# A transformer block on one core: the second output projection by seven products instead of eight

## The chip, the cores and the metric

The kernel runs on one core of one Trainium2 chip. The metric is the device time of one execution, in microseconds (us). A core has a matrix engine (TensorE, "PE" in the profile; "PEld" is its loading of the stationary operand), a vector engine (VectorE, "DVE"), a scalar engine (ScalarE, "ACT"), a general engine (GpSimd, "POOL") and a queue engine that here only issues transfers (SyncE, "SP"). PE reads from the on-chip memory SBUF and adds into PSUM, eight banks of 2 KB per partition, 128 partitions. [...]

## The reference

One block of a diffusion transformer, batch B = 2, N = 2048 tokens, C = 576 features, 16 heads of 36, hidden width 2304, all in float32. Cut to what matters:

```
mod = silu(c) @ w_ada + b_ada                      # six rows of 576 per sequence
xn  = layernorm(x) * (1 + sc_msa) + sh_msa
q, k, v = split(xn @ w_qkv + b_qkv);  q, k = layernorm per head
o   = softmax(q k^T * 36**-0.5) v                  # N x 576
x1  = x + g_msa * (o @ w_proj + b_proj)            # the output projection: the change is here
h   = gelu((layernorm(x1) * (1 + sc_mlp) + sh_mlp) @ w1 + b1)
out = x1 + g_mlp * (h @ w2 + b2)
```

## The kernel before, in words

The path that runs is block_of_small (the other one, for inputs whose scores may be large, is not taken). It does, for each of the two sequences b in turn, the input stage (q, k, v), the attention (attend, eight pairs of heads p, four blocks of 512 queries qb, four groups of keys g: steps (p, qb, g)), and the output projection (outputs). Then comes the MLP over both sequences: a first product whose inputs are 512 tokens by 576 features at a time, and a second product. Both MLP products already work by Strassen's scheme: a product of two 2 x 2 block matrices is made of seven block products instead of eight, of sums and differences of the blocks.

**The output projection before.** The attention leaves o transposed in SBUF, as held["qo"]: five chunks of features by 2048 tokens. Four chunks have 128 features each, and the last has the remaining 64, stored twice (partitions 0 to 63 and 64 to 127). w_proj lies in wp (four chunks of 128 rows by 576 columns) and wp4 (the last 64 rows: the left 288 columns on partitions 0 to 63, the right 288 on partitions 64 to 127). For a tile of 128 tokens, whole (L403 to L412) makes for each half a of the 576 output columns four matmuls with 128 rows of contraction, moving 288 columns (L406); halved (L414 to L419) makes one matmul of 64 rows per half, on the two halves of the PE array (L417). outputs (L1353) takes the 16 tiles of a sequence in groups of four: whole for two tiles, halved for all four, whole for the other two. Each tile has its own PSUM tile of two banks (pool "s", four buffers, so all eight banks).

Out of PSUM, DVE multiplies the tile by the gate g_msa (L1367, evicted) and adds the residual x1, which lies in DRAM as x + g_msa * b_proj and was put there during the attention (residual_begun, L1341, by GpSimd). The residual comes by a GpSimd-issued load (L1362), is added on DVE (L1380, summed), and goes back by a GpSimd-issued store (L1381). Seven of the eleven tiles "spare" serve as buffers for that, so a load waits for the store of seven tiles before.

**What else runs during the second projection.** The MLP's first product is prepared by a table `between`, keyed by the token tile at which placed(t) runs its entries:

```
for j in range(TPB + 1):
    between.setdefault(2 * j + 6, []).append(... turned_modulated(...))
for i, t in enumerate((6, 8, 10, 12)):
    between.setdefault(t, []).append(weight_sums[i])
    between.setdefault(t + 1, []).append(last_parts[i])
```

turned_modulated works on ACT (L1022, L388, L389) and ends with a subtraction on GpSimd (L390). weight_sums are four DVE operations on whole weight tiles (L1581 to L1584, 128 x 2304 elements); the first waits for weights wb that ACT's queue starts loading (L1565) once the attention's memory is free. last_parts are DVE operations on the last 64 rows (L400, L401, L1577).

**Order.** PE's order is the program's (a manual schedule around the whole block). In the second projection DVE's order is also the program's; ACT, SP and GpSimd are ordered by the scheduler. In attend, DVE, GpSimd and ACT stand in the program's order; hooks, keyed by (p, qb, g), place extra work in it. An engine carries out its own queue strictly in order: an instruction that waits holds all behind it.

**Around the stage.** Before it stand the last accumulations of the attention (L1291), and a last division: a reciprocal of the sums (L1260) that waits for a transfer (den), and a multiplication (L1261). After it, PE goes on with the first MLP product (L1655), whose first matmul waits for the last read of the projection's PSUM tiles; DVE makes token sums (L1625 to L1628).

Of the kernel before, what the change touches and what calls it, by code (L numbers as in the profile page):

```python
# [8 lines left out]
F32 = mybir.dt.float32  # L9
# [3 lines left out]
ALU = mybir.AluOpType  # L13
# [3 lines left out]
P = 128  # L17
# [5 lines left out]
FULL = 4  # L23
# [8 lines left out]
def dit_block(  # L32
# [25 lines left out]
    nc = tc.nc  # L58
    B, N, C = x.shape
# [3 lines left out]
    NT = N // P  # L63
    NPAIR = H // 2
    HALF = C // 2
# [20 lines left out]
    def s_tile():  # L86
        return psum["s"].tile([P, 2, 512], F32, tag="s", name="s")
# [8 lines left out]
    def opened(name, bufs=1, side="left"):  # L96

        stack = ExitStack()
        pool = stack.enter_context(tc.tile_pool(name=name, bufs=bufs, side=side, reuse_waits="tile"))
        return pool, stack.close  # L100

    def opened_psum(**bufs):

        stack = ExitStack()
        for n, count in bufs.items():
            psum[n] = stack.enter_context(
                tc.tile_pool(name=f"ps_{n}", bufs=count, space=PSUM, reuse_waits="tile")
            )
# [14 lines left out]
    def halves(ap):  # L123
        return ap.rearrange("p (a f) -> p a f", a=2)
# [15 lines left out]
    with tc.tile_pool(name="bound", bufs=1, side="right") as bound:  # L140
# [11 lines left out]
        product = bound.tile([1, 1], F32, name="product")  # L152
# [179 lines left out]
    x1_dram = dram.tile([B, N, C], F32, name="x1_dram")  # L332
# [419 lines left out]
    def block_of_small():  # L752
# [552 lines left out]
        def output_weights(b):  # L1305
            pool, close = opened("wp", side="right")
            wp = pool.tile([P, FULL, C], F32, name="wp")
            wp4 = pool.tile([P, 1, HALF], F32, name="wp4")
            nc.sync.dma_start(out=wp, in_=w_proj[0:512, :].rearrange("(k p) f -> p k f", p=P))
            last_chunk(wp4, w_proj, 1, HALF)  # L1310
            return (wp, wp4, gate_rows(pool, 0, b), pool), close


        def rows_begun(tiles):

            st = xs["pool"].tile([P, 2, 6], F32, name="st", bufs=2)
            mv = xs["pool"].tile([P, len(tiles), 2], F32, name="mvs", bufs=1)
            rstd = xs["pool"].tile([P, len(tiles)], F32, name="rstds", bufs=1)

            def load(i):  # L1320
                xt, src, _ = tiles[i]
                not_sooner(xt)
                nc.gpsimd.dma_start(out=xt, in_=src)

            def measure(i):
                for a in range(2):
# [12 lines left out]
            return load, measure, turn  # L1339
# [80 lines left out]
            summed()  # L1420


        close_psum = opened_psum(s=4)
        xnts, turned, loaded = {0: first_modulated()}, {}, {}

# [5 lines left out]
        for b in range(B):  # L1431
            work, close_work = opened("work", side="right")
            with tc.manual_schedule(
                engines={mybir.EngineType.DVE, mybir.EngineType.SP, mybir.EngineType.Pool}
            ):
                left = inputs(b, weights, making, work, xnts, turned, loaded)
            close_weights()
            close_work()
            close_outs = outs_opened()
            att, close_att = opened("att")  # L1440
            close_psum()
            close_psum = opened_psum(b=8)
            km[1] = att.tile([P, N // 2], F32, name="km1")
            qm[1] = att.tile([P, BLK], F32, name="qm1")
            opening = {}

            def ada_opened():
                opening["ada"], opening["close"] = opened("ada_later", 2, side="right")
                opening["was"] = ada_weights(opening["ada"], GATES[0])
                opening["gates"] = gate_biases(opening["ada"], GATES[0], GATES[2])  # L1450

            def ada_gates():
                gates(opening["was"], opening["gates"], *GATES[:2])
                opening["was"] = ada_weights(opening["ada"], LATER[0])
                opening["biases"] = feature_biases(opening["ada"], LATER[0], nc.sync)

            def ada_feature_rows():
                opening["rows"] = feature_rows(opening["ada"], opening["was"], opening["biases"])

            def ada_features():  # L1460
                features(opening["rows"], LATER[1])
                opening["close"]()

            def output_opened():
                opening["wp"] = output_weights(b)

            hooks = {
                (0, 0, 0): lambda: left,
                (4, 0, 1): output_opened,
            }  # L1470
            hooks |= {
                (3 + t // NBLK, t % NBLK, 3): lambda t=t: residual_begun(b, t) for t in range(NT + 1)
            }
            if b + 1 < B:
                begun = [(spare[5 + t], x[b + 1, t * P : (t + 1) * P, :], spare[8 + t]) for t in range(3)]

                def rows_opened():
                    opening["begun"] = rows_begun(begun)
                    for i in range(len(begun)):
                        opening["begun"][0](i)  # L1480

                def rows_turned():
                    opening["turned"] = opening["begun"][2]()

                hooks |= {(7, 1, 1): rows_opened, (None, None, None): rows_turned}
                hooks |= {
                    (7, 2 + i // NG, i % NG): lambda i=i: opening["begun"][1](i) for i in range(len(begun))
                }
# [12 lines left out]
            close_psum()  # L1501
            close_psum = opened_psum(s=4)
            wp, close_wp = opening["wp"]
            if b + 1 < B:
                weights, close_weights, making = kept_weights()
                xnts = {t: input_loaded(opening["turned"][t], nc.sync) for t in range(2)}
                turned, loaded = {2: opening["turned"][2]}, {}
                first = []

                def turned_of(t):  # L1510
                    squares = spare[8 + t % 3]
                    return (lambda x1: first.append(squares_turned(x1, nc.gpsimd, squares))) if t <= TPB else None

                with tc.manual_schedule(engines={mybir.EngineType.DVE}):
                    outputs(b, wp, {12: [lambda: input_modulated(b + 1, xnts[0])]}, spare[:8], turned_of)
# [84 lines left out]
            between.setdefault(t + 1, []).append(last_parts[i])  # L1600
        in_order = tc.manual_schedule(engines={mybir.EngineType.DVE})
        in_order.__enter__()
        outputs(B - 1, wp, between, spare[:7])
        close_wp()
        close_outs()
        close_xs()
# [296 lines left out]
```

## Time and profile before

| | |
|---|---|
| time, three runs | 3149.82 us median (3149.64 to 3151.75) |
| the profiled execution's own time | 3152.0 us |
| span of its instructions | 3150.2 us, 46743 instructions |
| PE busy | 3125.2 us, 99% of the span |
| DVE, ACT, POOL busy | 1515.6 us (48%), 1471.2 us (47%), 664.2 us (21%) |
| granted PE clock | 0.999 of full speed |
| second projection, PE | from 2076.76 to 2148.47 us of the span |
| first matmul of the MLP after it | 2149.36 us |

Read it from PE: it is busy for all but some 25 us of the span, so time is saved by giving PE less to do, and lost by making PE wait. In the trace each float32 matmul stands as two entries, so a count of 64 in a timeline is 32 matmul instructions. A "mean" of a matmul is the length of one that overlaps its neighbours; what a matmul costs is the distance between starts.

### The profile page before, as it was taken

The page shows a single profiled execution, that of the slowest core. Times are in us where ns is not written, and L with a number is a line of the kernel's source. Part 1 is how long each engine was busy: PE and PEld are TensorE (multiplying, and loading weights), DVE is VectorE, ACT ScalarE, POOL GpSimd, SP SyncE. Part 2 cuts the span into 40 slices and gives each one's busy share as a digit, 9 for nine tenths or more (in the row PEclk, how much of TensorE's full clock was granted, in tenths as well). Part 3 has the DMA queues.
Part 4 walks back from the last instruction along what each step waited for, and adds up shares of the span by engine and source line. Part 5 has one row for each costly group of instructions (what it writes and reads, how often), then busy time and mean ns, then how long its engine had stood idle before and what let it go on. Part 6 is the DMA issues. An engine that isn't in the chain of part 4 may idle for free. (4 is left out here: it accounts for less than half of the span.)

```text
span 3150.2 us, 46743 instructions
## 1 busy us (share of the span) xinstructions
PE 3125.2 (99%) x17553; PEld 1862.0 (59%) x17553; DVE 1515.6 (48%) x2181; ACT 1471.2 (47%) x2843; POOL 664.2 (21%) x932
## 2 busy tenths in 40 slices
PE   8999999999999999999999999999999999999999
PEld 5883333333333788633333333368888888777777
DVE  6653443444344556434443444445566554545454
ACT  2326666666666122466666666633555541000000
POOL 4641000011110455200011111013333320112111
PEclk9999999999999999999999999999999999999999
DMA  5753221132221756411122222146554434333331
GB/s 142 179 96 95 78 64 46 54 80 73 65 74 41 244 101 123 88 45 34 44 62 68 81 65 66 56 159 188 166 132 137 136 109 165 106 121 117 117 105 39
DMA packets 300451, 311.94 MB, mean 99 GB/s; under 512 B 178936, under 2 KB 233080, under 8 KB 298104
## 3 DMA queue, kind: packets, MB, share of 16 engines
q1 hardware_dynamic: 252240, 192.19, 21.2%
q0 software_dynamic: 44432, 111.07, 13.3%
q10 hardware_dynamic: 3544, 5.60, 0.5%
q8 instruction: 141, 2.31, 0.3%
q14 instruction: 94, 0.77, 0.1%
HBM read 191.80 MB, written 106.45 MB: 95 GB/s over the span
## 5 line engine op out<-in xcount | busy, mean ns | idle before, releaser
L1232 ACT ACTIVATE pt<-b 128x512 f32<-128x512 f32 x2048 | 1057.6, 610 | 484.2 <-PE b L1241 271.2
L1241 PE MATMUL b<-pt,vt 128*64 128x512 f32 x4096 | 935.0, 598 | 0.0
L1241 PEld LDWEIGHTS b<-pt,vt 128*64 128x64 f32 x4096 | 271.8, 136 | 582.1 <-issue 438.8
L1228 PE MATMUL b<-qm,km 32*128 32x512 f32 x4096 | 571.9, 614 | 1.0 <-issue 1.0
L1291 DVE TENSOR_TENSOR ot<-b,ot 128x512 f32<-128x512 f32 x192 | 132.8, 692 | 617.5 <-PE b L1241 617.5
L1228 PE MATMUL b<-qe,ke 16*128 16x512 f32 x2048 | 422.1, 788 | 0.0
L1101 PE MATMUL s<-wq,xnt 128*128 128x288 f32 x1536 | 404.9, 407 | 2.1 <-ACT xnt L395 2.1
L1228 PEld LDWEIGHTS b<-qm,km 32*128 32x128 f32 x4096 | 192.3, 184 | 276.8 <-ACT pt L1232 215.6
L1815 PE MATMUL s<-ws,as 128*128 128x288 f32 x1440 | 351.8, 406 | 0.0
L1101 PEld LDWEIGHTS s<-wq,xnt 128*128 128x128 f32 x1536 | 281.5, 190 | 64.7 <-ACT xnt L395 1.6
L1815 PEld LDWEIGHTS s<-ws,as 128*128 128x128 f32 x1440 | 273.6, 190 | 75.6
L1260 DVE RECIPROCAL den<-den 128x512 f32<-128x512 f32 x64 | 213.6, 3337 | 11.1 <-DMA den<-den_dram 11.1
L1655 PE MATMUL m<-xnt,wb 128*128 128x256 f32 x864 | 210.4, 379 | 1.6 <-issue 0.9
L1655 PE MATMUL m<-s,wb 128*128 128x256 f32 x864 | 210.0, 379 | 0.0
L1005 POOL DMA_DIRECT2D turned<-squares x212 | 142.5, 678 | 259.0 <-DVE squares L1000 241.0
L1655 PEld LDWEIGHTS m<-s,wb 128*128 128x128 f32 x864 | 164.2, 190 | 22.3
L1228 PEld LDWEIGHTS b<-qe,ke 16*128 16x128 f32 x2048 | 107.8, 184 | 115.9 <-issue 112.0
L1289 DVE COPY ot<-b 128x512 f32<-128x512 f32 x64 | 44.3, 692 | 272.7 <-PE b L1241 272.7
L1655 PEld LDWEIGHTS m<-xnt,wb 128*128 128x128 f32 x864 | 158.9, 190 | 21.3 <-issue 1.3
L1693 ACT ACTIVATE cs<-cs,b_sb 128x512 f32<-128x512 f32 x144 | 98.9, 719 | 111.8 <-DVE cs L1688 85.8
L812 POOL DMA_DIRECT2D km<-qk x56 | 28.2, 503 | 571.7 <-PE b L1228 568.8
L1022 ACT ACTIVATE xnt<-xnt,mod 128x128 f32<-128x128 f32 x244 | 100.4, 481 | 102.1 <-DMA xnt<-turned 94.6
(206 smaller groups left out, 2941.0 us busy)
## 6 DMA issues: line engine op xcount, KB each, us to landing
gelu<-cs SPq DMA_DIRECT2D x144, 256.0 KB
hidden<-gelu SPq DMA_DIRECT2D x16, 2304.0 KB
x_dram<-spare POOLq DMA_DIRECT2D x64, 288.0 KB, 2.5
qk<-turned_qk SPq DMA_DIRECT2D x120, 144.0 KB
qm<-qk SPq DMA_DIRECT2D x256, 64.0 KB
den<-den_dram SPq DMA_DIRECT2D x128, 128.0 KB
turned<-squares POOLq DMA_DIRECT2D x212, 72.0 KB, 2.5
xnt<-turned POOLq DMA_DIRECT2D x54, 256.0 KB, 4.1
```

What stands on the lines that cost most here:

```text
L1005: queue.dma_start(out=by_square[g], in_=squares[g * SQ : (g + 1) * SQ, :].rearrange("p (k j) -> p k j", j=SQ))
L1022: nc.scalar.activation(part, part, AF.Identity, **affine(which, k, b))
L1101: nc.tensor.matmul(out_a, full[:, k, :], wq[:, k, f], start=k == 0, stop=False)
L1228: nc.tensor.matmul(ps, k[r, keys], q[r, :], start=first, stop=not first)
L1232: nc.scalar.activation(pt[:, h, :], banks[2 * c + h], AF.Exp, scale=SCALE)
L1241: nc.tensor.matmul(acc[64 * h : 64 * h + 64, :], vt[:, v0 : v0 + 64], pt[:, h, :], start=pt is pts[0][0], stop=pt is pts[-1][0],)
L1260: nc.vector.reciprocal(den, den)
L1289: nc.vector.tensor_copy(ot, acc)
L1291: nc.vector.tensor_tensor(ot, acc, ot, ALU.add)
L1655: nc.tensor.matmul(out_m[m], wb[:, slot[m], k, f * P : (f + 1) * P], moving[m](k), start=k == 0 and m in (1, 2, 5, 6), stop=k == 1 and m == 1,
L1693: nc.scalar.activation(part, part, AF.Gelu, bias=b1_sb[:, g : g + 1])
L1815: nc.tensor.matmul(ms[m], stationary[m][:, f, :], ws[m][:, f, :], start=(f == 0), stop=(f == HF - 1))
```

## The change

The second sequence's projection (b = 1) is made by outputs_by_pairs instead of outputs; the first sequence's stays as it was.

A pair is two tiles of 128 tokens, a and b, so with the 512 full features in two halves of 256 and the 576 outputs in two halves of 288 there is a 2 x 2 by 2 x 2 block product. It is made of seven products of two matmuls each (14 per pair instead of 16). The 64 last features stay outside the scheme: two tiles of 64 rows in the first two matmuls of a pair (PSUM tiles x and y), and two at its end (PSUM tile z), these with a difference of the two token tiles' last rows. That is again four matmuls of 64 rows per pair.

- **Weights.** pair_weights loads w_proj and the gate at the same step of the attention as before. During attention steps p = 5 and 6 (11 hooks, one operation each), GpSimd multiplies the weights by the gate and makes five sums of weight blocks. The gate is so in the weights, and DVE no longer multiplies by it.
- **Token sums.** pair_summed makes, on GpSimd, five sums or differences of 128 x 256 elements and two of 64 x 128, per pair. Their memory (pair_memory) is one set for even pairs and one for odd, in tiles of the input stage. The sums of pairs 0 and 1 are made in the attention, at steps (7, 2, 3) and (7, 3, 0); those of pair p + 2 within pair p, into the memory that PE is just reading for pair p.
- **Out of PSUM.** Each pair has four PSUM tiles x, y, z, w of two banks. DVE adds their parts into the residual rows in SBUF, eight additions per pair: four of 576 columns and four of 288.
- **Residual rows.** Two token tiles at a time (576 KB), three buffers, so the load for pair p + 2 waits for the store of pair p - 1. GpSimd issues both, in the program's order with the sums: in pair p first the load for p + 2, then the sums for p + 2, then the store of p, which waits for DVE's last addition of pair p.
- **GpSimd's order** in this stage is now the program's, so the subtractions of turned_modulated (L390 before) stand in pairs 3 to 7, ahead of the load.

```diff
+        def pair_summed(dst, p):
+            q00, q01, q10, q11, a, b = pair_blocks(p)
+            for i, one, op, two in (
+                (2, q10, ALU.add, q11),
+                (5, q00, ALU.add, q01),
+                (1, q00, ALU.add, q11),
+                (7, q01, ALU.subtract, q11),
+                (6, q10, ALU.subtract, q00),
+            ):
+                nc.gpsimd.tensor_tensor(dst[i], one, two, op)
+            for r, one, two in ((slice(0, 64), a, b), (slice(64, P), b, a)):
+                nc.gpsimd.tensor_tensor(dst["last"][r], one[r], two[r], ALU.subtract)
...
+        def outputs_by_pairs(b, weights, memory, between, scratch):
...
+            def residual(p):
+                if p < pairs:
+                    rows[p] = scratch[p % len(scratch)]
+                    nc.gpsimd.dma_start(out=rows[p], in_=rows_of(x1_dram, p))
...
+            def product(out, tokens, i, start=True, stop=True):
+                for k in range(2):
+                    nc.tensor.matmul(
+                        out[:, :HALF],
+                        tokens[:, k, :],
+                        sums[i][:, k, :],
+                        start=start and k == 0,
+                        stop=stop and k == 1,
+                    )
+
+            def last_product(out, tokens, a, first=True):
+                r = slice(64 * a, 64 * a + 64)
+                nc.tensor.matmul(out[:, :HALF], tokens[r], last[r], start=first, stop=not first)
+
+            for p in range(3):
+                residual(p)
+            for p in range(pairs):
+                q00, q01, q10, q11, a, c = pair_blocks(p)
+                s = memory[p % 2]
+                x, y, z, w = (s_tile() for _ in range(4))
+                quarters = rows[p].rearrange("p t (a f) -> p (t a) f", a=2)
+                inner, outer = quarters[:, 1:3, :], quarters[:, 0::3, :]
+
+                def added(dst, part, op=ALU.add):
+                    nc.vector.tensor_tensor(dst, dst, part, op)
+
+                placed(2 * p)
+                last_product(x[:, 0, :], a, 1)
+                last_product(y[:, 1, :], c, 0)
+                product(x[:, 0, :], q00, 3, False)
+                product(x[:, 1, :], s[2], 2)
+                added(inner, x[:, :, :HALF])
+                added(quarters[:, 3, :], x[:, 0, :HALF])
+                added(quarters[:, 3, :], x[:, 1, :HALF], ALU.subtract)
+                product(y[:, 0, :], s[5], 5)
+                product(y[:, 1, :], q11, 4, False)
+                added(inner, y[:, :, :HALF])
+                added(quarters[:, 0, :], y[:, 0, :HALF], ALU.subtract)
+                added(quarters[:, 0, :], y[:, 1, :HALF])
+                product(w[:, 0, :], s[1], 1)
+                placed(2 * p + 1)
+                added(outer, w[:, 0, :HALF].unsqueeze(1).to_broadcast([P, 2, HALF]))
+                product(z[:, 0, :], s[7], 7, stop=False)
+                product(z[:, 1, :], s[6], 6, stop=False)
+                last_product(z[:, 0, :], s["last"], 0, False)
+                last_product(z[:, 1, :], s["last"], 1, False)
+                if p >= 1 and p + 2 < pairs:
+                    residual(p + 2)
+                if p + 2 < pairs:
+                    pair_summed(s, p + 2)
+                added(outer, z[:, :, :HALF])
+                nc.gpsimd.dma_start(out=rows_of(x1_dram, p), in_=rows[p])
...
+            if b + 1 == B:
+                hooks |= {
+                    (5 + i // 6, 1 + i % 6 // 2, 1 + i % 2): lambda i=i: opening["wp"][1][i]() for i in range(11)
+                }
+                hooks |= {(NPAIR - 1, 2, 3): lambda: pair_begun(0), (NPAIR - 1, 3, 0): lambda: pair_begun(1)}
...
-        outputs(B - 1, wp, between, spare[:7])
+        with tc.manual_schedule(engines={mybir.EngineType.Pool}):
+            outputs_by_pairs(
+                B - 1, wp, opening["pairs"], between, [held["spare"][:, 2 * i : 2 * i + 2, :] for i in range(3)]
+            )
```

More of the change, by code (lines that the diff above doesn't have):

```diff
@@ L1311, in output_weights, with pair_weights, gated, last_gated @@
             return (wp, wp4, gate_rows(pool, 0, b), pool), close
+        def pair_weights(b):
+            pool, close = opened("wp", side="right")
+            wp = pool.tile([P, FULL, C], F32, name="wp")
+            wp4 = pool.tile([P, 1, HALF], F32, name="wp4")
+            nc.sync.dma_start(out=wp, in_=w_proj[0:512, :].rearrange("(k p) f -> p k f", p=P))
+            last_chunk(wp4, w_proj, 1, HALF)
+            g1 = gate_rows(pool, 0, b)
+            left, right = (wp[:, :, a * HALF : (a + 1) * HALF] for a in range(2))
+            sums = {
+                1: pool.tile([P, 2, HALF], F32, name="sum1"),
+                2: left[:, 0:2, :],
+                3: right[:, 0:2, :],
+                4: left[:, 2:4, :],
+                5: right[:, 2:4, :],
+                6: pool.tile([P, 2, HALF], F32, name="sum6"),
+                7: halves(g1),
+            }
+            def gated(k):
+                nc.gpsimd.tensor_tensor(wp[:, k, :], wp[:, k, :], g1, ALU.mult)
+            def last_gated(a):
+                r = slice(64 * a, 64 * a + 64)
+                nc.gpsimd.tensor_tensor(wp4[r, 0, :], wp4[r, 0, :], g1[r, a * HALF : (a + 1) * HALF], ALU.mult)
+            def combined(i, one, op, two):
+                nc.gpsimd.tensor_tensor(sums[i], sums[one], sums[two], op)
+            making = [
+                *(lambda k=k: gated(k) for k in range(FULL)),
+                *(lambda a=a: last_gated(a) for a in range(2)),
+                lambda: combined(1, 2, ALU.add, 5),
+                lambda: combined(6, 2, ALU.add, 3),
+                lambda: combined(7, 4, ALU.add, 5),
+                lambda: combined(3, 3, ALU.subtract, 5),
+                lambda: combined(4, 4, ALU.subtract, 2),
+            ]
+            return (sums, wp4[:, 0, :]), making, close
@@ new lines, in pair_memory @@
+        def pair_memory():
+            fulls = [xs["pool"].tile([P, FULL, P], F32, name="xnt", bufs=3) for _ in range(3)]
+            fulls += [
+                xt[:, : FULL * P].rearrange("p (k n) -> p k n", k=FULL) for xt in xs["tiles"][:2]
+            ]
+            return [
+                {
+                    **{m: fulls[i][:, 2 * a : 2 * a + 2, :] for m, i, a in places},
+                    "last": xs["tiles"][n][:, FULL * P : (FULL + 1) * P],
+                }
+                for n, places in enumerate((
+                    ((1, 3, 0), (2, 3, 1), (5, 4, 0), (6, 4, 1), (7, 2, 0)),
+                    ((1, 0, 0), (2, 0, 1), (5, 1, 0), (6, 1, 1), (7, 2, 1)),
+                ))
+            ]
@@ new lines, in pair_blocks @@
+        def pair_blocks(p):
+            qo = held["qo"]
+            a, b = (slice((2 * p + i) * P, (2 * p + i + 1) * P) for i in range(2))
+            return qo[:, 0:2, a], qo[:, 2:4, a], qo[:, 0:2, b], qo[:, 2:4, b], qo[:, FULL, a], qo[:, FULL, b]
+        def pair_summed(dst, p):
[10 more added lines that the diff above has]
+                nc.gpsimd.tensor_tensor(dst["last"][r], one[r], two[r], ALU.subtract)
@@ L1420, in outputs, with rows_of, placed @@
             summed()
+        def outputs_by_pairs(b, weights, memory, between, scratch):
+            sums, last = weights
+            pairs = NT // 2
+            rows = {}
+            def rows_of(ap, p):
+                return ap[b, 2 * p * P : 2 * (p + 1) * P, :].rearrange("(t p) c -> p t c", p=P)
+            def residual(p):
+                if p < pairs:
+                    rows[p] = scratch[p % len(scratch)]
+                    nc.gpsimd.dma_start(out=rows[p], in_=rows_of(x1_dram, p))
+            def placed(t):
+                for do in between.get(t, ()):
+                    do()
+            def product(out, tokens, i, start=True, stop=True):
[8 more added lines that the diff above has]
+            def last_product(out, tokens, a, first=True):
+                r = slice(64 * a, 64 * a + 64)
+                nc.tensor.matmul(out[:, :HALF], tokens[r], last[r], start=first, stop=not first)
[35 more added lines that the diff above has]
+                nc.gpsimd.dma_start(out=rows_of(x1_dram, p), in_=rows[p])
@@ L1464, in output_opened, with pair_begun @@
             def output_opened():
-                opening["wp"] = output_weights(b)
+                opening["wp"] = (output_weights if b + 1 < B else pair_weights)(b)
+            def pair_begun(p):
+                if p == 0:
+                    opening["pairs"] = pair_memory()
+                pair_summed(opening["pairs"][p], p)
             hooks = {
@@ L1473, in block_of_small @@
             }
+            if b + 1 == B:
+                hooks |= {
+                    (5 + i // 6, 1 + i % 6 // 2, 1 + i % 2): lambda i=i: opening["wp"][1][i]() for i in range(11)
+                }
+                hooks |= {(NPAIR - 1, 2, 3): lambda: pair_begun(0), (NPAIR - 1, 3, 0): lambda: pair_begun(1)}
             if b + 1 < B:
@@ L1502, in block_of_small @@
             close_psum = opened_psum(s=4)
-            wp, close_wp = opening["wp"]
+            wp, *_, close_wp = opening["wp"]
             if b + 1 < B:
```

## The prediction, made before the changed kernel ran

> **What bounds the kernel now.** I read the page first: the busy line of part 1, then the chain of waits.
>
> ```profile
> PE 3125.2 (99%) x17553; PEld 1862.0 (59%) x17553; DVE 1515.6 (48%) x2181; ACT 1471.2 (47%) x2843; POOL 664.2 (21%) x932
> PE 30%; DVE 0%; ACT 0%; issue 0%
> ```
>
> PE hardly waits anywhere, so only its own work, or a new wait of it, can move the time. Next the timeline of PE around the second projection; columns are start, length, engine, line, operation, count, and idle time before.
>
> ```profile
> 2076.76 8.03 PE L406 MATMUL s<-wp,qo 128*128 128x288 f32 x32 [0.82 <-DVE ot L1291]
> 2084.72 2.21 PE L417 MATMUL s<-wp,qo 64*128 64x288 f32 x16
> 2086.86 15.79 PE L406 MATMUL s<-wp,qo 128*128 128x288 f32 x64
> ...
> 2140.44 8.03 PE L406 MATMUL s<-wp,qo 128*128 128x288 f32 x32
> 2149.36 1.97 PE L1655 MATMUL m<-xnt,wb 128*128 128x256 f32 x8 [0.90 <-issue]
> ```
>
> The stage is packed: from 2076.76 to the MLP's start at 2149.36 are 72.6 us, of which 0.9 is the wait for DVE's last read of PSUM. The price of one entry comes from the chain, where 2016 of the same width follow each other:
>
> ```profile
> 2654.78 488.89 PE s L1815 x2016
> ```
>
> That is 0.2425 us. Entries of 64 rows run two at a time: 16 of them are 8 slots, 1.94 us at that price. A group of four tiles (72 slots, 17.46) takes 2102.58 - 2084.72 = 17.86 us, so going to the 64-row form and back costs 0.4.
>
> Then DVE, GpSimd and the transfers in the same stretch:
>
> ```profile
> 2083.36 3.35 DVE L1260 RECIPROCAL den<-den 128x512 f32<-128x512 f32 x1 [6.65 <-DMA den<-den_dram]
> 2106.07 2.56 DVE L1581 TENSOR_TENSOR wb<-wb 128x2304 f32<-128x2304 f32 x1 [1.24 <-DMA wb<-in_w_dram]
> 2111.66 1.35 DVE L401 TENSOR_TENSOR wr<-spare,wr 64x1152 fp32r<-64x1152 f32 x1
> ```
> ```profile
> 2096.64 1.22 POOL L1381 DMA_DIRECT2D x_dram<-spare  x2 [1.01 <-DVE spare L1380]
> 2104.07 0.54 POOL L1362 DMA_DIRECT2D spare<-x_dram  x1 [6.21 <-DMA x_dram<-spare]
> 2106.15 2.79 POOL L390 TENSOR_TENSOR parts<-tail,parts 128x128 fp32r<-128x128 f32 x1
> 2119.39 1.21 POOL L1381 DMA_DIRECT2D x_dram<-spare  x2 [2.33 <-DVE spare L1380]
> 2122.06 0.54 POOL L1362 DMA_DIRECT2D spare<-x_dram  x1 [1.46 <-DMA x_dram<-spare]
> ```
>
> Three things are to be seen. A reciprocal of the attention falls inside the stage, at 2083. A store lands in some 2.5 us at 2119, but in over 7 while the weights wb load (2096). And a GpSimd subtraction took 2.79 us while DVE added whole weight tiles. Its line gives the usual length, beside GpSimd's 576-wide addition, and two additions out of PSUM on DVE:
>
> ```profile
> L390 POOL TENSOR_TENSOR parts<-tail,parts x32: 447/468/2785, 2081.5 to 2576.6; 128x128 fp32r<-128x128 f32 x32
> L1350 POOL TENSOR_TENSOR spare<-spare x32: 1408/1416/1868, 586.5 to 1980.9; 128x576 f32<-128x576 f32 x32
> L1822 DVE TENSOR_TENSOR y<-y,s 128x288 f32<-128x288 f32 x16 | 7.3, 454 | 66.2 <-PE s L1815 66.2
> ```
>
> **What the Trainium skill says.** GPSIMD Engine Reference, section 3.1: an operation with two inputs runs at about 2.6 cycles an element at 1.2 GHz, so 2.2 ns. The trace agrees: 128 wide 0.46 us, 576 wide 1.41, a slope of 2.1 ns. SBUF — State Buffer, "Who interferes with whom": a DVE operation with two SBUF inputs and a GpSimd operation that reads SBUF shut each other out for a whole instruction; with one operand in PSUM they don't. The 2.79 above agrees; a subtraction lying wholly under an addition out of PSUM (L1115) took 0.46. DMA: Bandwidth & Descriptors, "Anatomy of one DMA": some 2.0 us and bytes at 436 GB/s, an estimate of 3.4 us for 590 KB. The trace's 295 KB took 2.1 to 2.3 us from the end of issue; I take 2.9 for a double one.
>
> **The change, part by part.**
>
> *PE's work.* Per pair 32 slots (14 matmuls are 28 entries, four of 64 rows are 4 slots) take the place of 36. Eight pairs: 256 x 0.2425 = 62.1. The 64-row form stands at a pair's end and the next one's start, so it is entered 9 times: 9 x 0.4 = 3.5. In all 65.6 against 71.4 before: 5.8 saved, if nothing waits.
>
> *Attention.* GpSimd gets eleven weight operations of at most 1.4 us (row L1350) and two sets of sums, ahead of need; the steps are 6 us long and GpSimd is busy 21%. What could cost: an operation with two SBUF inputs on DVE may start up to 1.4 us late, with DVE half idle. I take 0; bounds 0 and +1.
>
> *DVE.* Before, each tile cost two operations of 0.68 (starts of L1367 and L1380), 2.7 per pair. Now four of 576 columns at 0.68 and four of 288 at 0.37, two of which wait for the one before (0.1 each): 4.4 per pair. Pairs 3 to 6 add a weight sum (2.47 between starts) and last_parts (0.69 + 1.38; 1.28 in pair 5): 8.9, over PE's 8.2. All eight PSUM banks are used once per pair, so PE's first two instructions of the next pair wait for the additions out of x and y.
>   - Pair 1: the order of instructions puts the reciprocal ahead of y's third addition. It can't start before 2083.4 (its transfer), so y comes free at 2087.2, where PE asks at 2085.4: 1.9 us lost.
>   - Pairs 3 to 6: the first weight sum stands ahead of x's additions and waits for wb until 2106, where PE began the pair at 2103.6. From there the backlog stays, and GpSimd's sums shut DVE out of its SBUF-only work by up to 0.75 each. Following the queue, PE waits at the head of pairs 5, 6 and 7 for 2.2, 2.3 and 0.7: 5.1 us.
>
> *GpSimd.* A sum of 256 elements is not in the trace; between 0.46 and 1.41, by the slope 0.73, with dispatch 0.75. Bounds: 0.65 and 0.9. A set is 5 x 0.75 + 2 x 0.5 = 4.75. A pair has: load issue 0.6, set 4.75, store issue 0.6, and the next load waits until that store has landed, 2.9: 8.9 us, over PE's 8.2 even with nothing in the way. From pair 3 on comes the subtraction 0.46, and waits behind DVE's weight work of some 2. Followed through: store 0 at 2089.4, load 3 at 2093.1, store 1 at 2098.4 (landing 7 us later, under wb), load 4 at 2106.2, sums 4 held to 2108.6 by the weight sum, load 5 at 2119.1, load 6 at 2130.1, load 7 at 2142.9. The first sum for pair 7 is ready at 2144.3; PE asks at 2142.8: 1.6 us lost. The residual rows themselves come over 4 us before DVE adds them.
>
> *Moved.* ACT's fourth-row work (L389) now waits for GpSimd's subtractions one pair at a time, as they share one tail tile; the wb loads stand ahead of all but one of these waits, so they start as before. The last subtraction for the MLP's first block stands in pair 6 and is in time.
>
> *End.* The MLP's first matmul waits for the last addition, 0.9 as before. The loads that the MLP's first rows need are issued about a microsecond sooner after it; its one wait of 0.55 there may shrink. I take 0, bounds -0.5 and +1.
>
> *Sum.* 65.6 + 1.9 + 5.1 + 1.6 + 0.9 = 75.1 us against 72.6: **2.5 us longer**. The profiled execution took 3152.0, 1.8 more than its span and 2.2 more than the median; nothing outside the span changes, so I add to the median: 3149.8 + 2.5 = 3152.3.
>
> **The rivals.**
>   - *GpSimd keeps up.* If the shutting out costs nothing, or stores land at once, GpSimd never decides, and DVE's backlog is shorter: 1.9 + 1.6 us of waits, 70.0 us, 2.6 saved: 3147.2. For it: GpSimd is 21% busy on the page. Against: the 2.79, and the chain of 8.9 per pair.
>   - *GpSimd's chain sets the pace*, slower: from a sum of about 0.8 us, or a landing of 3.5, each pair from 5 on waits for its sums. With 0.9 per sum the same following gives 79.2 us: 6.6 lost, 3156.4, and more with contention. For it: five rounds in a row, each over PE's 8.2. Against: the sums are made a whole pair ahead.
>   - *Nothing waits.* 65.6 + 0.9, so 6.1 saved: 3143.7. Against it stands the reciprocal's fixed place in DVE's order.
>   - That PE's work isn't less is excluded by the instruction counts.
>
> **How the numbers follow.** The chances: forecast 0.48, GpSimd keeps up 0.27, GpSimd's chain 0.20, nothing waits 0.05. A measurement here can tell some 0.2%, 6.3 us, from no change. Below 3143.5 lies most of the last case, 0.04; above 3156.1 most of the chain case and a little of the forecast, 0.20; between them 0.76. The range 3146.5 to 3157.5 leaves out some 0.1 on each side; the forecast's own is 3149.5 to 3155.
>
> **What would show it.** In the timeline of the changed kernel: 256 slots between about 2077 and 2151; idle PE entries released by DVE at the head of pair 1 (about 2 us) and of pairs 5 to 7; one released by GpSimd in pair 7's second product; the GpSimd sums at 0.73 alone and longer beside the weight sums; loads 13 to 11 us apart. It is wrong if DVE's weight work starts long before or after 2106, if the sums take 0.9 or more, or if PE waits elsewhere.

## The result, and the profile after

The changed kernel takes 3154.11 us (median of 20 runs, 3151.86 to 3156.48); the kernel before, on the same chip, took 3149.51 (20 runs, 3148.12 to 3152.97). The ratio is 1.0015, 95% interval 1.0009 to 1.0020: some 4.6 us slower (2.8 to 6.3), less than the 0.2% that the prediction counted as a change. The forecast was 3152.3. Its size was near, but the traces show that the time was lost in other places than the forecast had it.

The first thing to read is the busy line of part 1 of the changed kernel's page, beside the one shown of before.

```profile
PE 3122.8 (99%) x17521; PEld 1856.8 (59%) x17521; DVE 1541.4 (49%) x2213; ACT 1471.6 (47%) x2843; POOL 719.2 (23%) x983
```

PE has 32 entries less (17553 before), and is busy 2.4 us less. Yet the span is 3152.3 us instead of 3150.2. Where it went is found by cutting PE's timeline at three of its instructions: the first matmul of the attention's scores, the second projection's first matmul, and the MLP's first matmul. What lies ahead of the first cut is left out, since it isn't touched and differs from run to run (the first score came at 240.40 us before and at 239.56 after; in later runs as early as 237.30). These stretches account for 2.93 us of the 4.6; the rest, 1.7, is not explained.

| us of the profiled execution | before | after | difference |
|---|---|---|---|
| first score to the second projection | 1836.36 | 1839.28 | +2.92 |
| second projection to the MLP's start | 72.60 | 71.46 | -1.14 |
| MLP's start to the end | 1000.85 | 1002.01 | +1.16 |
| together | 2909.81 | 2912.74 | +2.93 |

**The second projection is shorter.** PE's timeline of the changed kernel, as before with start, length, engine, line, operation and idle time before:

```profile
2078.84 0.76 PE L1530 MATMUL s<-wp,qo 64*128 64x288 f32 x4 [0.87 <-issue]
...
2088.46 0.75 PE L1530 MATMUL s<-wp,qo 64*128 64x288 f32 x2 [0.70 <-DVE spare L1542]
...
2121.20 0.99 PE L1530 MATMUL s<-wp,qo 64*128 64x288 f32 x4
...
2131.50 0.75 PE L1530 MATMUL s<-wp,qo 64*128 64x288 f32 x2 [0.77 <-DVE spare L1542]
...
2142.60 2.21 PE L1520 MATMUL s<-wp,xnt 128*128 128x288 f32 x8 [0.72 <-POOL xnt L1386]
...
2150.30 1.97 PE L1817 MATMUL m<-xnt,wb 128*128 128x256 f32 x8 [0.93 <-issue]
```

From the first L1520 of one pair to that of the next are 9.61, 8.16, 8.16, 8.16, 8.51, 10.06 and 8.46 us. A pair without a wait takes 8.16, so the heads of pairs 1, 5, 6 and 7 cost 1.45, 0.35, 1.90 and 0.30. (The idle times in brackets are less than that: a break costs PE more than the idle time that the record shows.) Within pair 7 the wait for GpSimd's sum costs 0.99. That is 5.0 us of waits, and 0.93 at the MLP's start.

DVE and GpSimd in the same stretch, the lines that answer to those of before, first DVE:

```profile
2084.75 3.34 DVE L1260 RECIPROCAL den<-den 128x512 f32<-128x512 f32 x1
...
2106.21 2.56 DVE L1740 TENSOR_TENSOR wb<-wb 128x2304 f32<-128x2304 f32 x1 [0.35 <-DMA wb<-in_w_dram]
...
2112.75 1.49 DVE L401 TENSOR_TENSOR wr<-spare,wr 64x1152 fp32r<-64x1152 f32 x1
```

and GpSimd:

```profile
2099.71 0.72 POOL L1569 DMA_DIRECT2D x_dram<-spare  x1
2107.85 0.71 POOL L1512 DMA_DIRECT2D spare<-x_dram  x1 [7.42 <-PE s L1520]
...
2125.87 2.86 POOL L390 TENSOR_TENSOR parts<-tail,parts 128x128 fp32r<-128x128 f32 x1
```

The reciprocal follows DVE's work without waiting for den. The first weight sum finds wb almost there (0.35 us). On GpSimd the second load waits 7.42 us behind the store of pair 1, which lies among wb's loads; the record names a long finished PE operation, since the store's landing was the last of several things that the load waits for. And L390 takes 2.86 us while DVE adds weights, as before.

**The attention of the second sequence is longer.** PE falls behind in three steps of 0.91 us, near 1816, 1841 and 1938 us of the span. The timeline around the second of them, in the changed kernel:

```profile
1834.30 0.57 POOL L1424 DMA_DIRECT2D spare<-in_x_dram  x1 [19.20 <-DVE met L791]
1834.88 1.42 POOL L1427 TENSOR_TENSOR spare<-spare 128x576 f32<-128x576 f32 x1
...
1837.16 2.78 POOL L1333 TENSOR_TENSOR wp<-wp,gate 128x576 f32<-128x576 f32 x2
1837.29 3.21 DVE L1261 TENSOR_TENSOR ot<-ot,den 128x512 f32<-128x512 f32 x1
...
1840.43 0.68 DVE L1291 TENSOR_TENSOR ot<-b,ot 128x512 f32<-128x512 f32 x1
...
1841.16 0.18 PEld L1228 LDWEIGHTS b<-qm,km 32*128 32x128 f32 x1 [0.64 <-DVE ot L1291]
```

And the same place in the kernel before:

```profile
1837.06 0.69 DVE L1261 TENSOR_TENSOR ot<-ot,den 128x512 f32<-128x512 f32 x1
...
1839.02 0.69 DVE L1291 TENSOR_TENSOR ot<-b,ot 128x512 f32<-128x512 f32 x1 [1.26 <-PE b L1241]
```

The reader sees a chain. GpSimd's queue stood at a load until DVE's copy L791, so the weight operations of two hooks had gathered behind it. From there load, addition and store take GpSimd to 1837.16, and the reciprocal ahead of the division takes DVE to 1837.26. So the two weight operations, back to back (x2, 2.78 us), meet the division. DVE's multiplication by the reciprocal, which has two inputs in SBUF, starts at 1837.29 and ends at 1840.50, 0.56 us after the second of them (1839.95): 3.21 us instead of 0.69. Behind it in DVE's queue stands L1291, which empties a PSUM bank; it comes 1.2 us later than before (1840.43 less 1839.02, less the 0.2 us by which this run is behind there), and PE waits for that bank. The same multiplication took 3.23 at 1812.43 and 3.18 at 1933.93, the other two places. Beside a single GpSimd operation of 1.4 us it took 1.82 and 1.89, and PE lost nothing. A fourth place also has two operations in a row:

```profile
1862.01 2.03 POOL L1337 TENSOR_TENSOR wp<-wp,gate 64x288 f32<-64x288 f32 x2
1862.14 1.24 DVE L1261 TENSOR_TENSOR ot<-ot,den 128x512 f32<-128x512 f32 x1
```

The first ends at 1862.82 and the second starts 0.08 us later, at 1862.90. Here the division got in between: it ended at 1863.38, again 0.56 us after the first, and the second operation took 1.14 us for the first one's 0.81. In the other three places the record has the second operation begin 0.04 to 0.07 us before the first one's end.

**The MLP's start is later still.** PE's second block there waited 0.55 us before, for DVE (L1689). Now:

```profile
2166.34 1.99 PE L1817 MATMUL m<-xnt,wb 128*128 128x256 f32 x8 [1.81 <-DVE cs L1851]
```

DVE's queue has the normalization of the next rows (L272 and on) ahead of that L1851. The timeline of the changed kernel shows what it waited for:

```profile
2148.76 9.75 SPq L1887 DMA_DIRECT2D ws<-in_w_dram  x3
...
2151.20 1.12 POOL L984 DMA_DIRECT2D xt<-x_dram  x2
...
2160.79 0.82 DVE L272 BATCH_NORM_STATS2 st<-xt 128x6 f32<-128x288 f32 x2 [8.05 <-DMA xt<-x_dram]
```

The rows xt land 9.6 us after their issue; before, issued at 2151.42, they were there at 2158.59, 7.2 us later. Two things had come ahead of them: three loads of the second MLP weights (ws, 1.33 MB each), which began at 2150.66 before, and a last store that is now 576 KB long.

### The profile page after: what moved, and what is told of

Read it like the earlier page. It is cut to its first block, busy times and chain, and to the rows that moved or that the text cites. A ratio compares the mean times of both kernels' runs of the same rounds, so it can differ in the third digit from the quotient of the medians.

```text
span 3152.3 us, 46789 instructions
## 1 busy us (share of the span) xinstructions
PE 3122.8 (99%) x17521; PEld 1856.8 (59%) x17521; DVE 1541.4 (49%) x2213; ACT 1471.6 (47%) x2843; POOL 719.2 (23%) x983
## 4 chain that ended last, share of the span: by engine, by line
PE 96%; POOL 1%; issue 1%; DMA 1%; DVE 0%; ACT 0%; POOLq 0%; ACTq 0%
PE b L1241 29%; PE b L1228 20%; PE s L1977 16%; PE s L1101 12%; PE m L1817 12%; PE m L1831 2%; PE s L406 2%; PE one L1817 2%; PE s L1103 2%; POOL xnt L1386 0%; PE s L1520 0%; DMA xt<-x_dram 0%; PE s L417 0%; DMA x_dram<-spare 0%; PE b L192 0%
## 5 line engine op out<-in xcount | busy, mean ns | idle before, releaser
L1291 DVE TENSOR_TENSOR ot<-b,ot 128x512 f32<-128x512 f32 x192 | 132.7, 691 | 611.5 <-PE b L1241 611.3
L1424 POOL DMA_DIRECT2D spare<-in_x_dram x32 | 17.5, 548 | 598.7 <-DVE met L791 583.1
```

Of the source, the lines that this page charges most:

```text
L1291: nc.vector.tensor_tensor(ot, acc, ot, ALU.add)
```

## The experiments

Eight kernels were run. In most of them the numbers of lines shift by a few. The table gives the same three stretches for all of them, from each one's profiled execution, and the measured median beside the kernel before on the same chip. (The eight ran on three chips, so the medians are compared with the one in brackets and not among themselves.)

| run | score to projection | projection | MLP to end | together, against before | median (before) | ratio, 95% interval |
|---|---|---|---|---|---|---|
| changed kernel | 1839.28 | 71.46 | 1002.01 | +2.93 | 3154.11 (3149.51) | 1.0009 to 1.0020 |
| e1_weights_spaced | 1836.38 | 72.04 | 1002.82 | +1.42 | 3151.46 (3149.28) | 0.9999 to 1.0015 |
| e2_division_later | 1839.21 | 79.20 | 1002.03 | +10.64 | 3160.37 (3149.28) | 1.0021 to 1.0049 |
| e3_w2_loads_later | 1839.15 | 71.59 | 1000.45 | +1.37 | 3151.27 (3149.28) | 1.0000 to 1.0017 |
| e4_rows_by_SP | 1839.15 | 71.21 | 1002.28 | +2.83 | 3151.85 (3149.28) | 0.9998 to 1.0015 |
| e5_division_later_wb_held | 1839.25 | 76.48 | 1001.85 | +7.77 | 3156.50 (3149.54) | 1.0014 to 1.0034 |
| e6_all_four | 1836.37 | 69.56 | 1000.96 | -2.92 | 3146.41 (3149.54) | 0.9984 to 1.0000 |
| e7_no_weight_sums | 1839.21 | 68.49 | 1003.41 | +1.30 | 3150.44 (3149.54) | 0.9993 to 1.0010 |
| e8_refined | 1836.34 | 67.19 | 1000.82 | -5.46 | 3144.44 (3149.52) | 0.9977 to 0.9990 |

The first stretch tells two values apart, 1836.4 and 1839.2, to 0.1 us. The projection repeats to 0.1 where its code is the same (71.46 and 71.59); the MLP's stretch is less steady (1001.85 to 1003.41 in the kernels that leave its code alone). Against the kernel before, medians and stretches agree within 0.9 us in the eight kernels, and differ by 1.7 in the changed kernel itself. So the verdicts below rest on the stretches and their lines; a median that lies 2 us under the changed kernel's 3154.11 is not yet a gain.

**1. The weight operations one by one.** Each of them gets a write or a read of one element on DVE ahead of it, so GpSimd can't start it before DVE has come to that step, far from the division.

```diff
...
             def gated(k):
+                nc.vector.tensor_copy(met, wp[0:1, k, 0:1])
                 nc.gpsimd.tensor_tensor(wp[:, k, :], wp[:, k, :], g1, ALU.mult)
...
-                    (5 + i // 6, 1 + i % 6 // 2, 1 + i % 2): lambda i=i: opening["wp"][1][i]() for i in range(11)
+                    (4 + (2 + i) // NBLK, (2 + i) % NBLK, 1): lambda i=i: opening["wp"][1][i]() for i in range(10)
```

> GpSimd's eleven weight operations are held one by one until VectorE has passed the second step of a query block (ten places, the two half ones together, from the fourth head pair on), so that none runs beside the division by den. Theory 1: the changed kernel lost 2.7 us in attention because two such operations back to back shut the 0.69 us division out for 3.2 us, three times, and each time PE waited 0.9. Then no division takes over 2.2 us, PE loses under 0.3 us against the kernel before in attention, and the whole is 2.7 us less than the changed kernel: about 3151.4. Rival: it is the mere number of GpSimd operations in attention, wherever they stand; then at least 2 of the 2.7 us stay, about 3153.5 or more.

The stretch took 1836.38 us, the kernel before 1836.36. The division near 1835 in DVE's timeline of this run:

```profile
1834.69 0.69 DVE L1261 TENSOR_TENSOR ot<-ot,den 128x512 f32<-128x512 f32 x1
1836.64 0.69 DVE L1291 TENSOR_TENSOR ot<-b,ot 128x512 f32<-128x512 f32 x1 [1.26 <-PE b L1241]
```

The longest of all 64 divisions was 1.91 us. All the operations are still there, so their number costs nothing; the loss came from where they stood. It is shown: the three steps, 2.75 us of the changed kernel's 2.92 there, are this collision. (The other 0.15 lie near 1303 us, where nothing was changed.) As a whole this kernel wins less than the 2.7 us of the theory: its projection took 0.58 us longer than the changed kernel's and its MLP 0.81, so the three stretches together are 1.5 us shorter. The median agrees with the theory's 3151.4, which the stretches don't. Why part was lost again wasn't followed up.

**2. The last division later.** The prediction had pair 1's wait in DVE's order: the reciprocal ahead of the third addition out of y. Here ot and den of the last query block lie in memory that outlives the attention, and the division is called after y's additions of pair 0.

```diff
-                den = pool.tile([P, BLK], F32, name="den")
+                den = opening["last"][1] if ending(p, qb) else pool.tile([P, BLK], F32, name="den")
...
+        between.setdefault(1, []).extend(opening["rest"])
```

> The last reciprocal and division of the attention are placed after the additions out of y of pair 0 (their two tiles lie elsewhere). Theory 1: the wait at the head of pair 1 goes (its first product now starts 9.6 us after pair 0's, then 8.2), and what follows moves up with it: 1.4 us less than the changed kernel, 3152.7. Rival: the pace of pairs 5 to 7 is set by VectorE's weight sums, which start when wb lands (2106) whatever PE does; then PE comes 1.4 us earlier to pair 5 and waits there 1.4 us longer, and the time doesn't change: 3154.1.

Neither came. The head of pair 1 no longer waits (8.16 us after pair 0's), but PE stands still later in it: pair 2 begins 15.03 us after it, 6.87 more than without a wait. From the timeline of this run:

```profile
2077.01 16.92 ACTq L1731 DMA_DIRECT2D wb<-in_w_dram  x4
...
2078.67 5.27 SPq L1260 DMA_DIRECT2D xt<-den_dram  x2
...
2088.62 3.35 DVE L1263 RECIPROCAL xt<-xt 128x512 f32<-128x512 f32 x1 [5.43 <-DMA xt<-den_dram]
...
2093.51 2.26 PE L1527 MATMUL s<-sum,xnt 128*128 128x288 f32 x4 [3.80 <-DVE spare L1549]
```

The tiles that the division used had been memory of the attention that wb goes into. With them elsewhere, wb's loads (4.7 MB) start at 2077.01 instead of 2095.57, ahead of den; den's issue takes 5.27 us instead of 1.09, and the reciprocal starts 11.9 us after the stage's first matmul (2076.72). In the changed kernel it was 5.9 (2084.75 after 2078.84). A wait on memory had kept a large load out of the way of a small one. Of the 6.87 us some 4.1 are PE's wait for DVE behind that reciprocal. The other 2.8 are PE's clock: the trace has it at 0.50 of full speed from 2092.41 to 2099.24, and the entries of a matmul start 0.48 us apart there instead of 0.24. No such stretch falls into this stage in the changed kernel; what brings it on was not tested.

**3. The same with wb held until den is there.**

```diff
+        def weights_begun():
+            for i in range(4):
+                nc.vector.tensor_copy(wb[0:1, i, 0, 0:1], opening["last"][1][0:1, 0:1])
+            for i, (k, f) in enumerate(((0, 0), (0, 1), (1, 0), (1, 1))):
+                nc.scalar.dma_start(...)
...
+        between.setdefault(1, []).extend([weights_begun, *opening["rest"]])
```

> As e2_division_later, but the loads of wb are held until den has landed, so they don't run ahead of it. Theory 1: the 7.7 us that e2_division_later lost in the stage came from wb's loads, which began 18 us sooner beside den's. Then den lands at about 2084 again, no wait of 3.8 us is left in pair 1, wb lands some 8 us earlier than in the changed kernel (near 2098), the head of pair 1 doesn't wait, and the stage takes 68.5 to 70 us (changed kernel 71.46): 1.5 to 3 us less than the changed kernel in all. Rival: the order of the division is itself what costs (the additions out of w and z stand behind it): a wait of 2 us or more stays in pair 1, and the stage takes 72 us or more.

den landed as expected, the reciprocal started at 2083.59, 6.75 us into the stage, and no wait is left in pairs 1 to 3 (8.16 us each). So the order of the division is not what costs. But the stage took 76.48 us, and what came in is a rival of the prediction, that GpSimd's chain sets the pace:

```profile
2109.55 0.94 POOL L1519 DMA_DIRECT2D spare<-x_dram  x1 [6.80 <-DMA x_dram<-spare]
...
2123.38 1.24 PE L1527 MATMUL s<-wp,xnt 128*128 128x288 f32 x4 [2.09 <-POOL xnt L1393]
...
2126.41 2.29 PE L1527 MATMUL s<-wp,xnt 128*128 128x288 f32 x4 [1.79 <-POOL xnt L1393]
```

The wb loads now lie over the stores of pairs 0 and 1. GpSimd waits 6.7 and 6.8 us for the two to land before it may issue the next load, and its sums stand behind that load. In pairs 4, 5 and 7 PE waits for the sums; in pair 5 a weight sum on DVE (2122.89, 2.89 us) stretches them further, five in 5.82 us instead of 3.47. Pair 5 takes 15.03 us, and some 2.5 of that are again the clock, at 0.50 from 2124.58 to 2131.41.

**4. The loads of ws held.**

```diff
+            nc.vector.memset(ws[m][0:1, 0, 0:1], 0.0)
             nc.sync.dma_start(out=ws[m], in_=quarter.rearrange("(f p) c -> p f c", p=P))
```

> The loads of the second MLP weights (ws), which begin at 2148.8 in the changed kernel, are held one by one behind VectorE's later work. Theory 1: the 1.8 us wait of PE's second block of the MLP comes from the rows xt landing 9.6 us after their issue among these loads; alone they land in some 3, and the wait falls to 0.5 or less: 1.3 to 1.8 us less than the changed kernel, about 3152.5. Rival: the store of 576 KB just ahead of the rows delays them, or they are late for another reason: they land over 8 us after issue and the wait stays at 1.8.

```profile
2154.57 0.82 DVE L272 BATCH_NORM_STATS2 st<-xt 128x6 f32<-128x288 f32 x2 [3.68 <-DMA xt<-x_dram]
```

Issued at 2149.36, the rows are there 5.2 us later, not 9.6, and PE's wait of 1.81 is gone altogether. The stretch from the MLP's start is 1.56 us shorter than in the changed kernel, and 0.40 shorter than in the kernel before. The 5.2 are more than the 3 of the theory; what remains has the 576 KB store ahead of it, and wasn't split further.

**5. Residual rows by SP.**

```diff
-                    nc.gpsimd.dma_start(out=rows[p], in_=rows_of(x1_dram, p))
+                    queue = nc.gpsimd if p < 3 else nc.sync
+                    queue.dma_start(out=rows[p], in_=rows_of(x1_dram, p))
```

> The residual rows of pairs 3 to 7 are loaded by SP's queue instead of GpSimd's, so GpSimd doesn't wait until a store has landed. Theory 1: GpSimd gains some 3 us per pair, the sums of pair 7 are there in time, and the 0.9 us wait in pair 7's second product goes: 0.9 us less than the changed kernel. Rival: VectorE's backlog sets the pace of pairs 5 to 7, and sums that come earlier only meet it elsewhere; the waits at the heads of pairs 5 to 7 and at the MLP's start take up what is won: no change.

The wait in pair 7's product went, as theory 1 has it: from its first to its last matmul the pair took 6.65 us instead of 7.64. But the heads of pairs 5 and 6 now cost 1.57 and 1.45 us instead of 0.35 and 1.90, and the stage took 71.21 us against 71.46. The rival holds for the time: GpSimd's chain wasn't what paced these pairs. (The median is 2.3 us under the changed kernel's, but the three stretches differ by 0.1 in all, so the edit didn't gain that.)

**6. No weight sums.** ScalarE copies a tile where DVE subtracted two, so part of the MLP is computed from other weights.

```diff
-            lambda: nc.vector.tensor_tensor(wb[:, 4], wb[:, 1], wb[:, 0], ALU.subtract),
+            lambda: nc.scalar.copy(wb[:, 4], wb[:, 1]),
...
```

> The four sums of the MLP's weights are left out: ScalarE copies one of the two instead, so the output isn't the reference's. Theory 1: VectorE's backlog in pairs 3 to 7 comes from these sums of 2.5 us. Then the waits at the heads of pairs 5, 6 and 7 (0.35, 1.9 and 0.3 us) go, GpSimd's operations of 1.9 to 3.2 us shrink to the usual length, the sums of pair 7 come in time, and the stage is 3 to 3.5 us shorter than in the changed kernel, near 68. Rival: pairs 5 to 7 wait for GpSimd's chain of sums, stores and loads, not for VectorE: at least half of these waits stays.

The distances of the pairs became 9.61 and then 8.16 five times and 8.26. What these distances lose before pairs 5, 6 and 7, 2.55 us in the changed kernel, is 0.10 here, and the wait within pair 7 fell from 0.99 to 0.47: together 2.97 us of stage. GpSimd's slow operations in these pairs show the cause from the other side. In the changed kernel, in pair 6:

```profile
2134.01 3.18 POOL L1388 TENSOR_TENSOR xt<-qo 64x128 f32<-64x128 f32 x2
```

and the same sums without DVE's weight sums:

```profile
2131.74 0.98 POOL L1388 TENSOR_TENSOR xt<-qo 64x128 f32<-64x128 f32 x2
```

So DVE's weight sums set the pace of pairs 5 to 7, directly, and in pair 7 in part through GpSimd. (The MLP's longer stretch in this run, 1003.41, wasn't followed up.)

**7. Together.** Kernels 1, 3 (with last_rows loaded ahead of wb), 4 and 5 in one, and last_parts moved from the pairs of the weight sums to pairs 1, 2, 3 and 7.

```diff
...
-            between.setdefault(t + 1, []).append(last_parts[i])
+            between.setdefault((3, 5, 7, 14)[i], []).append(last_parts[i])
...
```

> Weight operations spaced (as e1), division later with wb held, ws loads held (as e3), residual rows by SP (as e4), and the last parts of the MLP weights in pairs 1, 2, 3 and 7 instead of 3 to 6. Theory 1: the losses stand each in its own place and add up: attention 0 against the kernel before, stage 66.5 to 68 us (before 72.6), MLP from its start to the end 0.4 us shorter than before. In all some 5 us less than before: 3144 to 3145.5. Rival: VectorE or the transfers pace the stage whatever is relieved: stage 70 us or more, 3147 or more.

The attention is at 1836.37, the losses there and at the MLP's second block are gone, and the kernel is 3.1 us under the kernel before, with an interval that reaches 1.0000. The stage, 69.56, lies between the two theories, and so does the whole. All pairs take 8.16 to 8.29 us but for one, whose head costs 2.97:

```profile
2106.09 3.12 DVE L1557 TENSOR_TENSOR spare<-spare,s 128x576 f32<-128x576 f32 x6 [2.97 <-DMA spare<-x_dram]
...
2107.76 0.75 PE L1545 MATMUL s<-wp,qo 64*128 64x288 f32 x2 [1.19 <-DVE spare L1557]
```

Pair 3's residual rows are late: they lie among wb's loads. Later PE waited 0.97 us once more, 92 us into the MLP, where a whole ws load ran beside a GELU store.

**8. Refined.** wb held until pair 1's additions are done, pair 3's rows by GpSimd ahead of it, weight sums one pair later, last_parts in pairs 1 to 3, ws in twelve pieces.

```diff
-        for i, t in enumerate((6, 8, 10, 12)):
+        for i, t in enumerate((8, 10, 12, 14)):
             between.setdefault(t, []).append(weight_sums[i])
-            between.setdefault(t + 1, []).append(last_parts[i])
+            between.setdefault((3, 5, 5, 7)[i], []).append(last_parts[i])
+        between.setdefault(1, []).extend(opening["rest"])
+        between.setdefault(4, []).append(weights_begun)
...
```

> As e6_all_four, with wb held until the additions of pair 1 are done and the rows of pair 3 loaded by GpSimd ahead of it, the weight sums in pairs 4 to 7 and the last parts in pairs 1 to 3, and the ws loads in twelve pieces of 442 KB, one per pair of MLP blocks. Theory 1: the 2.4 us that PE waited at the head of pair 4 in e6_all_four came from the rows of pair 3, which landed late among wb's loads, and the 1.0 us in the MLP from a whole ws load beside a GELU store; both go. Stage 66.5 to 67.5 us, MLP 0.5 to 1 us shorter than before, attention 0: 6 us less than before, 3143 to 3144. Rival: VectorE's weight sums in the last four pairs still hold PE, or the rows of pair 4 land late instead: stage 69 us or more, 3146 or more.

From the stage's first matmul to 2300 us PE's timeline of this run marks three waits:

```profile
2074.37 0.76 PE L1545 MATMUL s<-wp,qo 64*128 64x288 f32 x4 [0.87 <-issue]
...
2141.57 1.97 PE L1840 MATMUL m<-xnt,wb 128*128 128x256 f32 x8 [0.93 <-issue]
...
2233.57 1.99 PE L1840 MATMUL m<-xnt,wb 128*128 128x256 f32 x8 [0.79 <-DVE ws L1911]
```

Six of the seven distances are 8.16 us; the one before pair 5, where the loading of a stationary operand waits for DVE's addition, is 8.88. The stage takes 67.19 us, 5.4 less than before, and the whole 3144.44 against 3149.52 (ratio 0.9983, 0.9977 to 0.9990), which beats both kernels. The MLP didn't become 0.5 to 1 us shorter than before, as expected, but 0.03 (1000.82). The third wait stayed, so smaller pieces of ws were not its cure (0.79 instead of 0.97). DVE's additions of that block had themselves waited for a store of the GELU's results to land:

```profile
2230.93 0.69 DVE L1867 TENSOR_TENSOR cs<-m,cs 128x512 f32<-128x512 f32 x1 [8.96 <-DMA gelu<-cs]
```

In the kernel before, the same wait was 7.12 us and PE lost nothing by it. Part of the gain, the ws loads, is not the change's: whether the kernel before would gain by it too wasn't tried.

## Why the prediction was right, step by step

The forecast of +2.5 us over before stands against +2.9 in the profiled executions and +4.6 (2.8 to 6.3) in the medians. That it came out near is luck. The forecast put the whole loss into the stage, 75.1 us against 72.6, and nothing into the attention and the MLP. The stage took 71.46: it became 1.1 us shorter, not 2.5 longer. Three errors, -3.64 in the stage, +2.92 in the attention and +1.16 in the MLP, add up to +0.44. By its own last sign, "or if PE waits elsewhere", its account of where the time goes was wrong. (Four of its sums are 0.1 off and cancel: 9 x 0.4 is 3.6, 2.2 + 2.3 + 0.7 is 5.2, 2087.2 less 2085.4 is 1.8, and 2144.3 less 2142.8 is 1.5.)

- *PE's work, 65.6 us.* Right: 71.46 less the waits (5.0 and 0.93) is 65.5, and a pair without a wait takes 8.16.
- *Attention, "I take 0; bounds 0 and +1".* This is the step that failed: +2.9. The prediction had the rule (a whole instruction shut out, "up to 1.4 us late") but priced one operation, "with DVE half idle". The hooks had put two on GpSimd's queue where an earlier wait let them run together, and they met DVE's division, which has two SBUF inputs and a PSUM release next behind it. Experiment 1 shows that the meeting is what costs.
- *Pair 1's wait, 1.9.* Right in place, 1.45 measured. The reciprocal didn't wait for den in this run: it started when DVE was free, at 2084.75.
- *Heads of pairs 5, 6 and 7, 5.1 in all.* The mechanism was right (experiment 6) and the size was twice too large: 0.35, 1.90 and 0.30, so 2.55. Two terms were over-priced, and no run parts them. One is the start of the first weight sum, forecast for 2106: it came at 2106.21, but 27.4 us after the stage's first matmul where 29.3 was meant, so DVE waited only 0.35 for wb. The other is the shutting out of DVE by GpSimd's sums, "up to 0.75 each": the four weight sums took 2.55 to 2.66 us, as without any, and L400 and L401 grew by at most 0.46 and 0.41 over their shortest (0.74 and 1.35). It was GpSimd that was held.
- *Pair 7's product, 1.6.* 0.99 measured; counted from the stage's first matmul (2078.84 here, 2076.76 before), the loads 3 and 4 came 0.6 and 0.4 us sooner than forecast and 5 to 7 came 2.9 to 4.2 sooner. One reading beside it was wrong: the residual rows didn't come "over 4 us before DVE adds them" in pair 7, where DVE waited 1.30 us for them (at 2144.89); PE's wait at the MLP's start stayed as it was.
- *MLP's start, "may shrink. I take 0, bounds -0.5 and +1".* It grew by 1.26, and the stretch by 1.16. The rows were indeed issued sooner, 0.9 us after the MLP's first matmul instead of 2.1; but the prediction left out that the ws loads begin sooner as well and run ahead of the rows. Experiment 4 shows it.
- *The rivals.* "GpSimd's chain sets the pace" isn't what the changed kernel does (experiment 5), but is largely what it does with the stores of two pairs under wb (experiment 3). "Nothing waits" is what experiment 8 comes close to.

The Trainium skill's rule (SBUF — State Buffer, "Who interferes with whom": the ports that the two share are an exclusive lock) is borne out in both directions: 0.69 becomes 3.21 on DVE, 0.98 becomes 3.18 on GpSimd. What the trace adds is that in three places a second GpSimd operation of the queue followed without letting the waiting DVE operation in; in the fourth, with 0.08 us between the two, it got in.

## What to carry to other kernels

Work that is put on an idle engine "ahead of need" runs when its queue lets it, not where the program has it: look for what it will meet there, several at a time, and hold it with a dependency where that matters. A load that is freed earlier can cost more than the wait that was removed, so ask of every removed wait which transfer it was holding back. And when a stage of 70 us is changed in a kernel of 3150, cut the trace at fixed instructions ahead of and behind it and compare the stretches: in the attention they told 0.1 us here, where the medians tell about 2.

## What the runs showed of the hardware

- A DVE multiplication with two SBUF inputs was kept out by two consecutive GpSimd operations together, 3.2 us for 0.69, in three places where the second began before the first had ended. Where 0.08 us lay between them it came in after the first, 1.24 us. In all of these it ended 0.56 us after the GpSimd operation that had kept it out.
- A store of 576 KB landed so that GpSimd went on 2.9 to 3.5 us after its issue had ended, and 6.7 to 7.6 us where 4.7 MB of weights were loading. Two loads of 295 KB took 5.2 us from issue to use behind one such store, and 9.6 with three loads of 1.33 MB ahead too.
- Issuing the two 64-partition transfers of den took SP 1.09 us, and 5.27 with wb's loads ahead.
- PE's granted clock fell to 0.50 for 6.83 us in experiments 2 and 3, each time while PE waited (3.80 us in one, 2.09 and 1.79 in the other), and entries of a matmul then started 0.48 us apart instead of 0.24. In experiment 7 PE waited 1.19 and 0.77 us at the head of a pair without such a fall.
